# Layer 3's gates, inner convolutions and last products as 64x64 row halves inside the first scores of a frame

## The chip, the core and the metric

The kernel runs on one core of a Trainium2 chip. The metric is the device time of one execution in microseconds, as the median over runs of the same program. The core has a matrix engine (PE, with its weight loads listed apart as PEld), a vector engine (DVE), an activation engine (ACT), a general engine (POOL) and an engine that only synchronises and issues transfers (SP). Each engine works through its own queue; semaphores tie them together. Matrix products land in eight PSUM banks of 128 partitions by 2 KB.

## The reference

A residual stream x of 8 blocks of 512 tokens by 128 channels runs through four layers, each an attention-like part and a feed-forward part, everything in float32. The change is in layer 3, whose work the kernel interleaves with layer 2's attention. Cut to these:

```python
# layer 2, attention: 16 heads of width 64, softmax over the queries' axis
scores = jnp.einsum('bhqp,bhkp->bhqk', q, k) / jnp.sqrt(jnp.float32(P))
attn = jax.nn.softmax(scores, axis=2)
ctx = jnp.einsum('bhqk,bhkp->bqhp', attn, v)
out = concat(ctx) @ l_w.T + l_b

# layer 3, first part: a causal depthwise convolution of 21 taps, then two 128x128 products
return input_data @ W1 + h_hatt @ W2 + bias

# layer 3, second part: every operand rounded to FP4 in groups of 16
gate = fp4_linear(x, w_gate)          # 128 -> 352
y = fp4_linear(x, w_up)               # 128 -> 352
h = jax.nn.silu(gate) * y
return fp4_linear(h, w_down)          # 352 -> 128
```

Each part adds its result to x, and takes a layer norm of x as its input.

## The kernel before

**Frames.** From about 660 us on, the program is one loop over 64 frames (function `late`). Frame n handles one pair of layer 2's heads for one block: n // 8 is the block, n % 8 the pair. A frame's order, written out by hand, is: `scores(n, 0)`, `context(n - 1)`, `scores(n, 1)`, `project(n)`. The Tile scheduler is off (`tc.manual_schedule()`), so each engine's queue is in the order in which the statements are written.

- `scores(n, half)` makes the scores of two tiles of 128 keys. Each key tile is four 64x64 matmuls of 512 columns into a double bank (pool "two", two of them). DVE takes the negative maximum (L1589, tile `nm`), and ACT two exponentials for each key tile (L1595, tile `ex`). A double bank is free again once its two exponentials are done.
- `context(n - 1)` is eight matmuls with 128 rows and 64 columns of weights (`ex,vs`).
- `project(n)` makes the queries and keys of two frames ahead (`xt,blob_a`), the values (`blob_a,xt`) and the output product of the frame before (`blob_a,ct`). It is already cut into row halves on 64x64 tiles: while rows 0 to 63 of one product run, rows 64 to 127 of another do. Two row halves of one product add into the same bank, so the second must not start before the first has ended. `mark` puts an empty instruction on SP that waits for the last matmul of the first half, and the second half's first matmul waits for that. A half there is at most eight matmuls. Its two wide results lie in the two banks of pool "one"; ACT empties the queries' bank (L1498, tile `q`) and DVE the keys' (L1499, tile `k`).

**Layer 3 in the frames.** `planned(b, f0_)` hangs the steps of block b into the frames from f0_ on. A step has a place in its frame: "P" lies on PE behind both key tiles of `scores(n, 0)`, on ACT between the exponentials of its two key tiles; "V" comes after `scores(n, 0)`, "G" after `context`, "D" ahead of `project`, "E" at the end of the frame. Block b starts every eight frames, so the steps of two or three blocks lie in one frame. Blocks 0 to 5 run wholly in frames; the later steps of block 6 and all of block 7 are in `end()`, written out by hand behind the loop.

The steps that the change touches, in before:

- `gated(j)`, P, four times a block: gate and up product of one tile of 128 tokens, each one 128x128 matmul of 352 columns (L247, `wt_gate,xt` and `wt_up,xt`) into two banks of "one". ACT's tanh (L1884) reads the gate, `gated_v` on DVE (L1890, L1894) reads both.
- `conv_out`, E, once a block: eight matmuls of 128 columns into one bank, `xp` with W1 and `acc` (the taps' sum) with W2, then `added` on DVE (L1831), the next layer norm's `stats2` and, a place later, `scale2` on ACT (L1435).
- `turn_h(i)`, P, twice: transposes of the 352 columns of `h` in chunks of 128, 128 and 96 (L1925), and two copies for each tile of tokens on ACT (L1928, L1931).
- `down`, P, once: twelve matmuls of 128 columns (`wd,ht`) into one bank, then `added` and the store.

The PE list of one such frame reads: two key tiles, [P steps], context, two key tiles, project, [E steps].

Of the kernel before, what the change touches and what calls it, by code (L numbers as in the profile page):

```python
# [25 lines left out]
P = 128  # L26
D = 128
# [134 lines left out]
def body(ctx, tc, dram, spans, x_in, ib, it, ic, ei, out):  # L162
# [1176 lines left out]

    I3 = 352  # L1340
    chunks = [(0, P), (1, P), (2, I3 - 2 * P)]

    def fp4_scale(pool, src, blocks, bufs=1, room=None):

# [42 lines left out]
    def late():  # L1387
# [11 lines left out]
        with tc.tile_pool(name="a2", bufs=2) as wp, tc.tile_pool(name="l3", bufs=1) as lp:  # L1399
# [94 lines left out]
            def queries_out(n, pk, pq):  # L1494
# [4 lines left out]
                nc.vector.tensor_scalar(k, pk, a2["kb"][:, cc : cc + 1], None, ALU.add)  # L1499
                qks[n] = q, k  # L1500

            def project(n):

                b, cc = divmod(n + 1, 8)
                b2, cc2 = divmod(n + 2, 8)
                bo, co = divmod(n - 1, 8)
                pk, pq, pv = bank(), bank(), bank("c")
                pv = pv.rearrange("p (j n) -> p j n", j=J)
                if co == 0:
                    outs[bo] = bank("o")  # L1510
                po = outs[bo].rearrange("p (j d) -> p j d", j=J)
                ct, xq, xv = cts.pop(n - 1), xts[b2], xts[b]

                after = []

                def put(*args, **kw):
                    ins = nc.tensor.matmul(*args, **kw).ins  # L1517
                    if after:
                        tc.add_manual_dep(ins, after.pop().name, SYNC)
                    return ins  # L1520

                def mark(ins):

                    m = nc.sync.nop(nofuse=True).ins
                    tc.add_manual_dep(m, ins.name, SYNC)
                    return m

                def wide(ps, w, r, first):
                    for m in range(2):
                        at_ = cc2 * P + 64 * m  # L1530
                        put(
                            ps[64 * m : 64 * (m + 1), :],
                            a2[w][r, at_ : at_ + 64],
                            xq[r, :],
                            start=first,
                            stop=not first,
                        )

                def by_tokens(ps, src, w, r, start, stop):
                    for j in range(J):  # L1540
                        for m in range(2):
                            at_ = j * P + 64 * m
                            last = put(
                                ps[64 * m : 64 * (m + 1), j, :],
                                src[r, at_ : at_ + 64],
                                w[r, :],
                                start=start and j == 0,
                                stop=stop and j == J - 1,
                            )
                    return last  # L1550

                low, high = slice(0, 64), slice(64, P)
                wl, wv = cols(a2["l"], co), cols(a2["v"], cc)
                wide(pk, "k", low, True)
                one = mark(by_tokens(po, ct, wl, high, co == 0, False))
                wide(pq, "q", low, True)
                two = mark(by_tokens(pv, xv, wv, high, True, False))
                after.append(one)
                wide(pk, "k", high, False)
                by_tokens(po, ct, wl, low, False, co == 7)  # L1560
                after.append(two)
                wide(pq, "q", high, False)
                by_tokens(pv, xv, wv, low, False, True)
                queries_out(n + 2, pk, pq)
                if co == 7:
                    add_to_residual(bo, po)
                values_out(n + 1, pv)

            def scores(n, half, between=lambda: None):


                q, k = qks[n]
# [8 lines left out]
                for kt in tiles:  # L1581
                    ps = bank2()
                    for i in range(2):
                        r = slice(64 * i, 64 * (i + 1))
                        for m in range(2):
                            at_ = kt * P + 64 * m
                            mm(ps[64 * m : 64 * (m + 1), i, :], k[r, at_ : at_ + 64], q[r, :])
                    nm = wp.tile([P, 2], F32, tag="nm", name="nm", bufs=4)
                    nc.vector.tensor_reduce(nm, ps, AX.X, ALU.max, negate=True)  # L1589
                    made[kt] = ps, nm  # L1590
# [170 lines left out]
            def layer3(b, xp, tile_, part=(0, J), conv_bank="one", h_tag="h"):  # L1761
# [111 lines left out]
                def gated(j, at_end=False, thirds=True):  # L1873
# [6 lines left out]
                        pg, pu = two[:, 0, :], two[:, 1, :]  # L1880
                    mm(pg[:, :I3], cols(t["xt"], j - j0), wt["gate"])
                    mm(pu[:, :I3], cols(t["xt"], j - j0), wt["up"])
                    s = lp.tile([P, I3], F32, tag="s", name="s", bufs=2)
                    nc.scalar.activation(s, pg[:, :I3], AF.Tanh, scale=0.5)  # L1884
                    if at_end and thirds:
# [33 lines left out]
                def turn_h(i):  # L1919
                    h = tile_("h", h_tile)  # L1920
                    ht = tile_("ht", lambda: lp.tile([P, J, 3, P], F32, tag="ht", name="ht"))
                    for j in (2 * i, 2 * i + 1):
                        pt = bank()
                        for k, w in chunks:
                            nc.tensor.transpose(  # L1925
                                pt[:w, k * P : (k + 1) * P], h[:, j, k * P : k * P + w], ident
                            )
                        nc.scalar.copy(  # L1928
                            ht[:, j, :2, :], pt[:, : 2 * P].rearrange("p (i n) -> p i n", i=2)
                        )  # L1930
                        nc.scalar.copy(ht[:96, j, 2, :], pt[:96, 2 * P : 3 * P])  # L1931

                def down():
                    ht = tile_("ht", None)
                    po = bank()
                    for j in range(j0, j1):
                        for k, w in chunks:
                            mm(
                                cols(po, j),
                                ht[:w, j, k, :],  # L1940
                                wt["down"][:w, k, :],
                                start=(j == j0 and k == 0),
                                stop=(j == j1 - 1 and k == 2),
                            )
                    added(po)
                    nc.sync.dma_start(
                        out[b * TB + lo : b * TB + hi, :].rearrange("(j p) d -> p j d", p=P),
                        x[b][:, j0:j1, :],
                    )

                stats, scale, turn_, _ = norm_steps(
                    b, lambda: xp()[:, pad + lo : pad + hi], "b3", part
                )
                stats2, scale2, _, t2 = norm_steps(b, None, None, part)
                return SimpleNamespace(**{k: v for k, v in locals().items() if callable(v)})

            def planned(b, f0_):

# [1 line left out]


                soon = b < 2 or b == NB - 2
                z = 9 - soon
                plan = [
                    (1, "V", s.stats) if b < 2 else (0, "E", s.stats),
                    (1, "G", s.scale),
                    (1, "E", s.turn_),
                    (2, "V", lambda: s.conv_v(1, 2, 3, 4)),
                    (2, "G", lambda: s.conv_s(6, 7)),
                    (2, "E", lambda: s.conv_s(8, 9, 10)),  # L1970
                    (2, "D", lambda: s.conv_v(5)),
                    (3, "G", lambda: s.conv_s(11, 12)),
                    (3, "E", lambda: s.conv_s(13, 14, 15)),
                    (4, "G", lambda: s.conv_s(16, 17)),
                    (4, "E", lambda: s.conv_s(18, 19, 20)),
                    (5, "V", s.join),
                    (5, "E", s.conv_out),
                    (5, "E", s.stats2),
                    (6, "G", s.scale2),
                    (6, "E", s.quant_x1) if soon else (7, "V", s.quant_x1),  # L1980
                    (z - 1, "V", s.quant_x2),
                    (z - 1, "E", s.turn_x),
                ]
                for j in range(J):

                    g = z + j + int(b > 0 and j > 0)
                    plan.append((g, "P", lambda j=j: s.gated(j)))
                    plan.append((g, "V", lambda j=j: s.gated_v(j)))
                plan += [
                    (z + 2, "V", lambda: s.quant_h1(0)),  # L1990
                    (z + 3, "V", lambda: s.quant_h2(0)),
                    (z + 4, "V", lambda: s.quant_h1(1)),
                    (z + 5, "V", lambda: s.quant_h2(1)),
                    (z + 5, "P", lambda: s.turn_h(0)),
                    (z + 6, "P", lambda: s.turn_h(1)),
                    (z + 6, "E", s.down) if b > NB - 4 else (z + 7, "P", s.down),
                ]
                for frame, kind, f in plan:
                    at(f0_ + frame, kind, f)
                return s  # L2000
# [100 lines left out]
            def weights_in_frames():  # L2101
# [20 lines left out]
                def turned_w(name):  # L2122
                    ps = bank()
                    w_ = wq[name]
                    if name == "down":
                        for i, w in chunks:
                            nc.tensor.transpose(
                                ps[:w, i * P : (i + 1) * P], w_[:, i * P : i * P + w], ident
                            )
                        wt["down"] = const.tile([P, 3, P], F32, tag="wd", name="wd")  # L2130
                        nc.vector.tensor_copy(
                            wt["down"][:, :2, :], ps[:, : 2 * P].rearrange("p (i n) -> p i n", i=2)
                        )
                        nc.vector.tensor_copy(wt["down"][:96, 2, :], ps[:96, 2 * P : 3 * P])
                    else:
                        for i, w in chunks:
                            nc.tensor.transpose(
# [67 lines left out]
            with tc.manual_schedule():  # L2205
# [1 line left out]
                xts[0] = t[0]["next"]  # L2207
                queries(0)
                for n in range(N):
                    scores(n, 0, lambda: (n > 0 or (values(0), queries(1)), hook(n, "P")))  # L2210
                    if n - 1 in experts_after:
                        waiting()
                    hook(n, "V")
# [63 lines left out]
```

## Time and profile before

| what | value |
|---|---|
| median of 3 runs | 1434.34 us (1434.13 to 1439.14) |
| the profiled execution's own time | 1434.78 us |
| its span, first to last instruction | 1433.0 us |
| mean granted PE clock | 0.998 |
| PE busy in the span | 1372.8 us (96%) |
| ACT, DVE, POOL busy | 1041.7, 986.5, 622.1 us |
| PE busy from 886 to 1287 us | 399.6 of 401 us |

A timeline row gives the start in microseconds, the time to the end of its last instruction, engine, line, operation, tiles (out<-in), the shape, and how many instructions were merged; in brackets the idle time ahead of it and what ended it. `64*64` is rows by columns of the weights. A float32 matmul shows as two records. Neighbouring PE rows overlap, because a matmul's record lasts longer than the time until the next one can start: what a piece of PE work costs is read from start to start.

### The profile page before, as it was taken

The numbers are of one execution on the slowest core, as the hardware profiler recorded it, in microseconds if no ns is written. First come the engines' busy times: TensorE is split into PE (matmuls) and PEld (weight loads), VectorE is DVE, ScalarE is ACT, GpSimd is POOL, SyncE is SP. The second block draws the span as 40 slices with busy tenths as digits, with TensorE's granted clock in tenths as the row PEclk, the third lists the DMA queues.
The fourth block names the chain that finished last, engine by engine and source line by source line (L and its number), as shares of the span: only waits on it lengthen the run. The fifth ranks groups of instructions, "written<-read, shape, count | busy, mean of one in ns | idle before, by whom it ended". The sixth has DMA issues, their size and how long they took to land.

```text
span 1433.0 us, 31909 instructions
## 1 busy us (share of the span) xinstructions
PE 1372.8 (96%) x12498; PEld 703.9 (49%) x12498; DVE 986.5 (69%) x2072; ACT 1041.7 (73%) x2126; POOL 622.1 (43%) x726
## 2 busy tenths in 40 slices
PE   7889999999999999999999899999999999999997
PEld 3752222222377745534553455555555555555566
DVE  6776665676477777634671687886887877877876
ACT  7869999999887646655875577876866767768632
POOL 6746766666533533201620272442632633524423
PEclk9999999999999999999999999999999999999999
DMA  5039999988451010101000000000000000000000
GB/s 176 1 49 132 140 133 129 126 129 124 77 181 42 10 41 24 39 1 31 2 2 1 1 2 9 2 2 9 2 2 9 1 9 2 2 9 2 2 8 16
DMA packets 33272, 60.06 MB, mean 42 GB/s; under 512 B 5601, under 2 KB 25633, under 8 KB 28642
## 3 DMA queue, kind: packets, MB, share of 16 engines
q1 hardware_dynamic: 32416, 56.18, 22.2%
q8 instruction: 99, 1.62, 0.5%
q10 hardware_dynamic: 578, 1.57, 0.3%
q14 instruction: 51, 0.42, 0.1%
q0 software_dynamic: 128, 0.26, 0.1%
HBM read 49.70 MB, written 8.29 MB: 40 GB/s over the span
## 4 chain that ended last, share of the span: by engine, by line
PE 65%; ACT 18%; DVE 11%; DMA 2%; issue 2%; POOL 1%; SPq 0%; DVEq 0%; POOLq 0%; ACTq 0%
PE ps L247 50%; PE ps L1517 13%; ACT hm L565 8%; ACT hm L564 4%; ACT ex L1595 3%; DVE nm L1589 2%; DMA gs<-gates 1%; DVE s L723 1%; ACT h L385 1%; DVE s L1423 1%; ACT xn L1435 1%; PE ps L1453 1%; DMA gates<-eq 1%; POOL rs L244 1%; DVE fa L1375 0%
## 5 line engine op out<-in xcount | busy, mean ns | idle before, releaser
L1595 ACT ACTIVATE ex<-ps,nm 128x512 f32<-128x512 f32 x512 | 345.6, 687 | 150.4 <-DVE nm L1589 150.4
L1589 DVE TENSOR_REDUCE nm<-ps 128x2 f32<-128x1024 f32 x256 | 299.6, 1211 | 46.2 <-PE ps L247 45.7
L247 PE MATMUL ps<-q,k 64*64 64x512 f32 x2048 | 250.6, 600 | 6.6 <-ACT ex L1595 5.5
L247 PE MATMUL ps<-ex,vs 128*64 128x512 f32 x1024 | 233.8, 598 | 0.0
L1517 PE MATMUL ps<-xt,blob_a 64*64 64x512 f32 x976 | 222.2, 589 | 0.0
L583 POOL TENSOR_TENSOR acc<-acc,pr 128x512 f32<-128x512 f32 x119 | 166.8, 1401 | 104.7 <-DVE pr L577 96.0
L1610 POOL TENSOR_TENSOR vs<-v,sm 128x256 f32<-128x256 f32 x128 | 78.4, 613 | 295.1 <-DVE sm L1609 268.9
L565 ACT ACTIVATE hm<-ps,blob_f 128x1536 f32<-128x1536 f32 x128 | 196.2, 1533 | 0.0
L577 DVE SCALAR_TENSOR_TENSOR pr<-ps,blob_f,gs 128x512 f32<-128x512 f32 x120 | 90.0, 750 | 88.9 <-PE ps L247 70.9
L247 PE MATMUL ps<-h,w 32*128 32x512 f32 x1024 | 147.4, 639 | 1.5 <-ACT hm L564 0.6
L247 PE MATMUL ps<-hm,w 128*32 128x512 f32 x1024 | 136.2, 604 | 2.0 <-DVE pr L577 2.0
L247 PEld LDWEIGHTS ps<-ex,vs 128*64 128x64 f32 x1024 | 67.8, 136 | 142.5 <-issue 116.5
L247 PEld LDWEIGHTS ps<-q,k 64*64 64x64 f32 x2048 | 68.1, 132 | 140.6 <-issue 78.6
L1797 POOL TENSOR_TENSOR acs<-acs,prod 128x512 f32<-128x512 f32 x98 | 124.9, 1274 | 8.5 <-ACT prod L1796 3.6
L1517 PE MATMUL ps<-blob_a,xt 64*64 64x128 f32 x1952 | 126.9, 269 | 0.0
L1517 PE MATMUL ps<-blob_a,ct 64*64 64x128 f32 x1952 | 126.8, 269 | 0.0
L1517 PEld LDWEIGHTS ps<-blob_a,ct 64*64 64x64 f32 x1952 | 113.7, 133 | 0.0
L1517 PEld LDWEIGHTS ps<-blob_a,xt 64*64 64x64 f32 x1952 | 110.3, 133 | 0.0
L243 POOL TENSOR_SCALAR rs<-mv 128x4 f32<-128x4 f32 (+1 forms) x69 | 17.8, 258 | 211.4 <-DVE mv L1425 140.2
L1595 ACT ACTIVATION_READ_ACCUMULATOR ex<-ps,nm 128x1 f32 x512 | 105.3, 206 | 0.0
L564 ACT ACTIVATE hm<-ps,blob_f 128x512 f32<-128x512 f32 x128 | 88.0, 687 | 17.5 <-PE ps L247 17.5
L247 PEld LDWEIGHTS ps<-h,w 32*128 32x128 f32 x1024 | 40.7, 183 | 109.0 <-ACT hm L564 93.9
(316 smaller groups left out, 2204.8 us busy)
## 6 DMA issues: line engine op xcount, KB each, us to landing
gs<-gates SPq DMA_DIRECT2D x256, 128.0 KB
blob_f<-in_f SPq DMA_DIRECT2D x1, 2560.0 KB
blob_a<-in_a SPq DMA_DIRECT2D x1, 2056.0 KB
x<-in_x SPq DMA_DIRECT2D x8, 256.0 KB
gates<-eq SPq DMA_DIRECT2D x8, 256.0 KB
ge<-gates SPq DMA_DIRECT2D x4, 512.0 KB
back<-nought SPq DMA_DIRECT2D x7, 256.0 KB
by_rows<-fxn SPq DMA_DIRECT2D x7, 256.0 KB
```

Of the source, the lines that this page charges most:

```text
L243: nc.gpsimd.tensor_scalar(t, var, EPS, None, ALU.add)
L244: nc.gpsimd.tensor_tensor(t, t, half[:, : t.shape[-1]], ALU.pow)
L247: nc.tensor.matmul(out_, lhs, rhs, start=start, stop=stop)
L564: nc.scalar.activation(hm[:, 0, :], p1, AF.Gelu, bias=bias)
L565: nc.scalar.activation(hm[:, 1:, :], p3, AF.Gelu, bias=bias)
L577: nc.vector.scalar_tensor_tensor(pr, po, f0["b2"][:, e : e + 1], gs, ALU.add, ALU.mult)
L583: nc.gpsimd.tensor_tensor(acc[:, b, :], acc[:, b, :], pr, ALU.add)
L1517: ins = nc.tensor.matmul(*args, **kw).ins
L1589: nc.vector.tensor_reduce(nm, ps, AX.X, ALU.max, negate=True)
L1595: nc.scalar.activation(ex[kt][:, i, :], ps[:, i, :], AF.Exp, bias=nm[:, i : i + 1], accum_out=sm[:, kt, i : i + 1],)
L1610: nc.gpsimd.tensor_tensor(vs[:, tiles, :, :], vs_[n][:, tiles, :].rearrange("p j (i n) -> p j i n", i=2), sm[:, tiles, :].unsqueeze(3).to_ ...
L1797: nc.gpsimd.tensor_tensor(t["acs"], t["acs"], p, ALU.add)
```

## The change

1. **Gates on 64x64 tiles.** A new place "S" in `scores(n, 0)`: the first half of a step is issued between the two key tiles, the second half behind the second. `gate_steps(j)` issues gate rows 0 to 63 and up rows 64 to 127 as the first half, up rows 0 to 63 and gate rows 64 to 127 as the second. `in_halves` puts one `mark` between them. The evaluation is now `gate_out` and stays in P.
2. **Convolutions of blocks 2 to 5** (`conv_steps`) and **last products of blocks 0 to 4** (`down_steps`) go the same way through `token_steps`: two banks of two token tiles each; the first half is all of rows 0 to 63 for tiles 0 and 1 and then all of rows 64 to 127 for tiles 2 and 3. Their sums are added by two DVE instructions (`pair_added`) in place of one.
3. **The 352 columns of h in three overlapping runs of 120**, with the doubled weight rows set to zero, so that a run splits into 64 and 56 rows; one ACT copy for each transposed tile in place of two.
4. **Other frames.** The inner convolution moves from the end of frame 5 to S of frame 6, its statistics to P and its scaling to E of frame 6; the first gate of inner blocks moves one frame later; `turn_h` and the last product of blocks 1 to 4 move one frame later; tap 4 goes from V to D of frame 2 and tap 5 from D of frame 2 to D of frame 3.

```diff
+            def in_halves(first, second):
+                def a():
+                    m = mark(first()[-1])
+                    def b():
+                        tc.add_manual_dep(second()[0], m.name, SYNC)
+                    return b
+                return a
...
-            def scores(n, half, between=lambda: None):
+            def scores(n, half, between=lambda: None, more=()):
...
                             mm(ps[64 * m : 64 * (m + 1), i, :], k[r, at_ : at_ + 64], q[r, :])
+                    more = [f() for f in more]
                     nm = wp.tile([P, 2], F32, tag="nm", name="nm", bufs=4)
...
+                def gate_steps(j):
...
+                    def first():
+                        t["gate", j] = pg, pu = bank(), bank()
+                        return rows_(pg, "gate", low, True) + rows_(pu, "up", high, True)
+                    def second():
+                        pg, pu = t["gate", j]
+                        return rows_(pu, "up", low, False) + rows_(pg, "gate", high, False)
+                    return in_halves(first, second)
+                def token_steps(name, terms):
+                    def rows_(ps, js, half, first):
+                        made = []
+                        for i, j in enumerate(js):
+                            for k, (src, w) in enumerate(terms()):
...
+                                for m in range(2):
+                                    made.append(
+                                        nc.tensor.matmul(
+                                            ps[64 * m : 64 * (m + 1), i * P : (i + 1) * P],
+                                            s_[r, 64 * m : 64 * (m + 1)],
+                                            w_[r, :],
...
+                    def first():
+                        t[name] = a, c_ = bank(), bank()
+                        return rows_(a, (0, 1), 0, True) + rows_(c_, (2, 3), 1, True)
+                    def second():
+                        a, c_ = t[name]
+                        return rows_(c_, (2, 3), 0, False) + rows_(a, (0, 1), 1, False)
+                    return in_halves(first, second)
...
-                    (2, "V", lambda: s.conv_v(1, 2, 3, 4)),
+                    (2, "V", lambda: s.conv_v(1, 2, 3)),
...
-                    (2, "D", lambda: s.conv_v(5)),
+                    (2, "D", lambda: s.conv_v(4)),
...
+                    (3, "D", lambda: s.conv_v(5)),
...
-                    (5, "E", s.conv_out),
-                    (5, "E", s.stats2),
-                    (6, "G", s.scale2),
+                if inner:
+                    plan += [
+                        (6, "S", s.conv_steps()),
+                        (6, "P", lambda: s.pair_added("conv")),
+                        (6, "P", s.stats2),
+                        (6, "E", s.scale2),
+                    ]
...
-                    g = z + j + int(b > 0 and j > 0)
-                    plan.append((g, "P", lambda j=j: s.gated(j)))
+                    g = z + j + int(inner or (b > 0 and j > 0))
+                    plan.append((g, "S", s.gate_steps(j)))
+                    plan.append((g, "P", lambda j=j: s.gate_out(j, *s.t["gate", j])))
...
-                    (z + 5, "P", lambda: s.turn_h(0)),
-                    (z + 6, "P", lambda: s.turn_h(1)),
-                    (z + 6, "E", s.down) if b > NB - 4 else (z + 7, "P", s.down),
+                    (z + 5 + w, "P", lambda: s.turn_h(0)),
+                    (z + 6 + w, "P", lambda: s.turn_h(1)),
...
+                        (z + 7 + w, "S", s.down_steps()),
+                        (z + 7 + w, "V", lambda: (s.pair_added("down"), s.stored())),
```

## The prediction

> **What bounds the kernel now.** I read the page first. Its first line puts PE far ahead of the others:
>
> ```profile
> PE 1372.8 (96%) x12498; PEld 703.9 (49%) x12498; DVE 986.5 (69%) x2072; ACT 1041.7 (73%) x2126; POOL 622.1 (43%) x726
> ```
>
> In the frames it is tighter still: 399.6 of 401 us from 886 to 1287. So time saved on PE in a frame counts in full, as long as no other engine is late. The timeline of PE, three stretches: a frame with a gate, one around an inner convolution (frame 38), one with a last product.
>
> ```profile
> 1020.76 1.90 PE L247 MATMUL ps<-q,k 64*64 64x512 f32 x16
> 1022.59 0.86 PE L247 MATMUL ps<-wt_gate,xt 128*128 128x352 f32 x2
> 1023.28 0.76 PE L247 MATMUL ps<-wt_up,xt 128*128 128x352 f32 x2
> 1023.97 3.65 PE L247 MATMUL ps<-ex,vs 128*64 128x512 f32 x16
> ...
> 1044.98 1.16 PE L247 MATMUL ps<-blob_l,xp 128*128 128x128 f32 x8
> 1045.98 1.06 PE L247 MATMUL ps<-blob_l,acc 128*128 128x128 f32 x8
> 1046.96 1.95 PE L247 MATMUL ps<-q,k 64*64 64x512 f32 x16
> 1048.84 0.87 PE L1925 MATMUL ps<-blob_c,h 128*128 128x128 f32 x6
> 1049.65 3.65 PE L247 MATMUL ps<-ex,vs 128*64 128x512 f32 x16
> ...
> 1072.94 2.94 PE L247 MATMUL ps<-wd,ht 128*128 128x128 f32 x24
> 1075.82 0.65 PE L247 MATMUL ps<-ex,vs 128*64 128x512 f32 x2
> ```
>
> Start to start, a gate costs 1023.97 - 1022.59 = 1.38 and a last product 2.88. Scores and context follow each other without a hole.
>
> ACT's timeline at two frame starts shows when the queries' bank comes free:
>
> ```profile
> 1020.99 0.69 ACT L1498 ACTIVATE q<-ps,qb 128x512 f32<-128x512 f32 x1
> ...
> 1033.32 0.70 ACT L1498 ACTIVATE q<-ps,qb 128x512 f32<-128x512 f32 x1
> ```
>
> That is 0.92 behind the first scores at 1020.76, and 1.24 behind those at 1032.78. Next, the weight loads inside a `project`, which tell how far PE looks ahead:
>
> ```profile
> 1006.49 0.47 PEld L1517 LDWEIGHTS ps<-blob_a,xt 64*64 64x64 f32 x8
> 1006.83 0.14 PEld L1517 LDWEIGHTS ps<-blob_a,ct 64*64 64x64 f32 x2
> 1006.93 0.14 PEld L1517 LDWEIGHTS ps<-xt,blob_a 64*64 64x64 f32 x2
> ```
>
> The `ct` pair is for rows 0 to 63, whose tiles could take new weights from 1006.56 on (start of the queries' second matmuls). It comes 0.27 later, with the last of the `xt` loads for rows 64 to 127, although those rows' own next loads wait till 1006.93. In program order, ten instructions ahead of the first `ct` load and thirteen ahead of the second were then unissued; one step (0.109) earlier, four more. The trace has the same offsets in all 52 `project`s. I read it as a window: an instruction overtakes at most thirteen unissued ones. Last, DVE in frame 38:
>
> ```profile
> 1047.07 0.69 DVE L1831 TENSOR_TENSOR x<-x,ps 128x512 f32<-128x512 f32 x1 [0.93 <-PE ps L247]
> 1049.06 2.35 DVE L1589 TENSOR_REDUCE nm<-ps 128x2 f32<-128x1024 f32 x2
> 1051.32 0.86 DVE L1423 BATCH_NORM_STATS2 s<-x 128x6 f32<-128x128 f32 x4
> 1055.54 2.32 DVE L1589 TENSOR_REDUCE nm<-ps 128x2 f32<-128x1024 f32 x2
> 1057.83 0.75 DVE L1499 TENSOR_SCALAR k<-ps,blob_a 128x512 f32<-128x512 f32 x1
> ```
>
> There DVE runs without a hole for eleven microseconds: in these frames it is the second bound.
>
> **Gates: 24 in frames.** `project` does four groups of 64x64 tiles by 512 columns in 3.46, so 0.866 a group and 0.595 for 352 columns; two halves 1.19 in place of 1.38: -0.19. But the first half stands one key tile (0.87) behind the frame's start where the old gate stood two behind it, and takes both banks of "one". Its up product gets the queries' bank, so its load waits for the copy at L1498 plus 0.10 (0.05 from an ACT end to the PE load released by it, as at the `xt` copy ending 753.73, and 0.05 for the load). Behind the waiting load PE's queue holds key tile 1, and the lag lasts to `context`, which needs all rows. With the copy ending at 0.92 the wait is 0.92 + 0.10 - 0.87 = 0.15; at 1.24, 0.47. Gate 0 of each block and gate 1 of block 0 find the bank free: 7 x -0.19 = -1.3. Gates 1 and 2 of blocks 1 to 5: 10 x (-0.19 + 0.15) = -0.4. Their gates 3, where the copy ends at 1.22 to 1.24 in every block: 5 x (-0.19 + 0.47) = +1.4. Block 0's gates 2 and 3, where ACT is later still (copies end 1.85 and 1.86 behind the scores at 806.83 and 820.40): about +0.8 and +0.4. Sum +0.9; the ends are -4.6 (no wait) and +2.5. The marker's way (0.15 from a record's end to SP's event at 1006.48) fits behind key tile 1, and no store stands ahead of it on SP: nothing.
>
> **Last products: 5.** Eight `project` matmul records in two columns take 0.435, so 0.109 a step. A half here is 24 records a row half, 12 steps, 1.31. If both row halves ran together: 2 x 1.31 = 2.62 against 2.88, -0.26. But all 48 instructions of rows 0 to 63 are queued first. Four issue per step, and the other rows' first load gets within thirteen unissued ones at the ninth step: 8 x 0.109 + 0.05 = 0.92 late. The same holds at each change of rows behind so long a run. From the frame's start: low rows 0.87 to 2.18, high rows from 1.79 to 3.10; key tile 1's low rows from 2.71 to 3.58; second half's low rows to 4.89, its high rows from 4.50 to 5.81. The two key tiles alone are 1.73, so the product costs 4.08: +1.2 each, +6.0 in all. Ends -1.3 and +6.5. The adds and the store move to V; DVE has holes in these frames (1.35 ahead of the old add).
>
> [...]
>
> **Inner convolutions: 4.** Here a row half has 32 instructions: the high rows start 4 x 0.109 + 0.05 = 0.49 behind the low ones, but their bank is the queries', whose copy at the end of frame 37 is late (ends 1.5 behind 1044.98). Counted from `project`'s last matmul (1044.81), with gate 3 having cost PE 0.3: bank free at 1.5; first half 0.87 to 2.37, key tile 1 to 3.24, second half to 4.2, context at 4.3. The old way: 1049.65 - 1044.81 less 0.80 of transposes, now a frame later, = 4.04. So PE alone +0.25. Then DVE: after key tile 1 it has a maximum (1.17), both adds (0.8), both statistics (1.3 each) and the rounding (2.9) ahead of the third maximum: 3.4 + 7.5 = 10.9, where the old row stands at 10.7 (1055.54) though PE is now 0.7 ahead. Two maxima and two pairs of exponentials (1.35 each) later the double banks come free at 13.6 and 14.9; PE wants them at 13.1 and 13.9. It stands in frame 39 some 0.5 and 0.5, where before it lost 0.33 (scores 2.16 at 1058.46 against 1.83). Context of frame 39 comes at 16.7, as before (16.6), but with 0.8 of transposes still to do: +0.85 in each of frames 30, 38 and 46. In frame 54 the other block's statistics are missing: +0.25. Sum +2.8; ends 0 and +5.
>
> **The rest.** Transposes keep count and columns. One ACT copy in place of two ends each `turn_h` about 0.1 earlier; in frames the exponentials hide that, in `end()` PE waits for it: -0.2 (0 to -0.4).
>
> **Sum.** +0.9 + 6.0 + 2.8 - 0.2 = +9.5 on the profiled execution's 1434.78 (span 1433.0 and 1.8 around it), which is 0.4 above the median: 1434.3 + 9.5 = 1443.8.
>
> **Rivals.**
> *The rows overlap in full* (the other side). The window is no limit for matmuls whose tiles are free. [...] For it: `ct` matmuls at 1006.99 do pass four waiting ones. Against: the constant offsets. Last products -1.3 in place of +6.0, convolutions +2.5: 1434.3 + 0.9 - 1.3 + 2.5 - 0.2 = 1436.2, not measurably slower.
> *The banks are free in time.* Gates save all 4.6: 1438.3 with the window, 1430.7 without. For it: PE waits nowhere for `q` in steady frames now. Against: the copy can't start before the queries' last matmul ends.
> *DVE and ACT fall further behind*, and stalls of 0.5 spread to two more frames a block: 1449.
> [...]
>
> **How the numbers follow.** Forecast 0.46; rows overlap 0.19, banks free 0.10, both 0.13; DVE 0.08; drains 0.04. A measurement of this kernel can tell about 0.5%, 7.2 us, from no change. Forecast alone spans 1439 to 1448: above 1441.5 with 0.34 of its 0.46; with the last two cases that makes slower 0.46. Of the 0.13 for both free, 0.11 is for convolutions and key tiles gaining too, below 1427.2: faster 0.11. The rest, 0.43, is the same. Range 1429 to 1449.
>
> **What would show it.** Right: `wd,ht` rows from first to second row half 0.9 apart, 4.1 a product; PE idle in front of `wt_up` ended by ACT `q`; scores behind frame 38 over 2.5. Wrong: both row halves of `wd,ht` starting within 0.1, or gate frames 0.19 shorter each.

## The result and the profile after

| | before | after |
|---|---|---|
| median | 1438.05 us (6 runs beside those of after) | 1445.06 us (6 runs, 1443.83 to 1450.06) |
| ratio | | 1.0064, 95% interval 1.0041 to 1.0087 |
| profiled execution | 1434.78 us, span 1433.0 | 1444.44 us, span 1442.3 |

The changed kernel is 0.6% slower: 9.66 us between the profiled executions, where 9.5 was predicted. Ahead of the first frame two executions can differ by over 5 us (it starts at 507.15 us in the trace of after, at 512.74 in that of `turns_by_term`), so a part is priced here inside the frames: from the start of one frame's `context` on PE to the start of the next, where untouched frames of two executions agree within 0.02 almost everywhere. From the first context to the last, after is 10.0 longer than before. (The first frame of the loop starts at 507.75 us in the trace of before, not at 660.)

The first line of the page after:

```profile
PE 1380.9 (96%) x13338; PEld 724.0 (50%) x13338; DVE 995.2 (69%) x2081; ACT 1042.1 (72%) x2094; POOL 624.0 (43%) x726
```

PE has 840 matmul records more and 8.1 us more work; DVE has 8.7 us more, ACT 0.4. PE's timeline, frame 37 (gate 3 of block 3) and frame 41 (the last product of block 3); lines have moved by 2 to 22 (L1500 is the old L1498, L1539 the old L1517):

```profile
1035.77 1.04 PE L247 MATMUL ps<-q,k 64*64 64x512 f32 x8
1036.63 0.76 PE L1978 MATMUL ps<-wt_gate,xt 64*64 64x352 f32 x4
1037.31 0.51 PE L1978 MATMUL ps<-wt_up,xt 64*64 64x352 f32 x2
...
1039.50 1.08 PE L247 MATMUL ps<-ex,vs 128*64 128x512 f32 x4
...
1086.87 1.09 PE L247 MATMUL ps<-q,k 64*64 64x512 f32 x8
1087.78 2.09 PE L2009 MATMUL ps<-wd,ht 64*64 64x128 f32 x42
...
1090.51 2.41 PE L2009 MATMUL ps<-wd,ht 64*64 64x128 f32 x48
1092.85 0.65 PE L247 MATMUL ps<-ex,vs 128*64 128x512 f32 x2
```

In frame 37 the gate's and the up product were to start together, as two products of `project` do (1005.28 and 1005.29 in before); the up product starts 0.68 later. The weight loads name what it waits for, ACT's copy of the queries, which ends 1.49 behind the scores (1.24 in before):

```profile
1036.56 0.70 ACT L1500 ACTIVATE q<-ps,qb 128x512 f32<-128x512 f32 x1
...
1037.31 0.14 PEld L1978 LDWEIGHTS ps<-wt_up,xt 64*64 64x64 f32 x2 [0.53 <-ACT q L1500]
```

In frame 41 a half should take 1.31, as worked out in the prediction. From its first record to the context the second half takes 2.34. A merged row has the form of its first instruction; by single records the 56-row matmuls start 0.886 behind the 64-row ones in both halves, and the first half keeps the upper rows from key tile 1 until 1090.02, 2.24 behind its own start.

Frame 38 holds a convolution. DVE's timeline behind it, and the scores of frame 39:

```profile
1052.89 0.74 DVE L2031 TENSOR_TENSOR x<-x,ps 128x256 f32<-128x256 f32 x2
1053.55 0.86 DVE L1425 BATCH_NORM_STATS2 s<-x 128x6 f32<-128x128 f32 x4
...
1054.80 0.86 DVE L1425 BATCH_NORM_STATS2 s<-x 128x6 f32<-128x128 f32 x4
...
1059.02 2.32 DVE L1605 TENSOR_REDUCE nm<-ps 128x2 f32<-128x1024 f32 x2
```

```profile
1061.75 1.09 PE L247 MATMUL ps<-q,k 64*64 64x512 f32 x8
1063.09 1.09 PE L247 MATMUL ps<-q,k 64*64 64x512 f32 x8 [0.25 <-ACT ex L1611]
```

```profile
1061.75 0.21 PEld L247 LDWEIGHTS ps<-q,k 64*64 64x64 f32 x8 [0.38 <-ACT ex L1611]
```

DVE works without a hole from the maximum at 1051.75 to the one at 1059.02, 10.71 behind the frame's scores (1048.31) and 10.81 behind the last matmul of `project` (1048.21), from which the forecast counted 10.9. The exponentials behind it release the double banks late: the load of frame 39's first key tile waits 0.38 for them, and its two key tiles stand 1.34 apart instead of 0.87.

### The profile page after: what moved, and what is told of

Read it like the earlier page. It is cut to its first block, busy times and chain, and to the rows that moved or that the text cites. A ratio compares the mean times of both kernels' runs of the same rounds, so it can differ in the third digit from the quotient of the medians.

```text
span 1442.3 us, 33570 instructions
## 1 busy us (share of the span) xinstructions
PE 1380.9 (96%) x13338; PEld 724.0 (50%) x13338; DVE 995.2 (69%) x2081; ACT 1042.1 (72%) x2094; POOL 624.0 (43%) x726
## 3 DMA queue, kind: packets, MB, share of 16 engines
q10 hardware_dynamic: 578, 1.57, 0.3%
## 4 chain that ended last, share of the span: by engine, by line
PE 65%; ACT 18%; DVE 11%; DMA 3%; issue 2%; POOL 1%; SPq 1%; DVEq 0%; POOLq 0%; ACTq 0%
PE ps L247 46%; PE ps L1539 12%; ACT hm L565 7%; ACT hm L564 3%; ACT ex L1611 3%; PE ps L1978 2%; PE ps L2009 2%; DVE nm L1605 2%; DMA gs<-gates 2%; DVE s L723 1%; ACT h L385 1%; ACT xn L1437 1%; DMA gates<-eq 1%; DVE s L1425 1%; SPq L545 1%
## 5 line engine op out<-in xcount | busy, mean ns | idle before, releaser
L247 PE MATMUL ps<-q,k 64*64 64x512 f32 x2048 | 265.1, 601 | 5.8 <-ACT ex L1611 4.5
L1539 PE MATMUL ps<-xt,blob_a 64*64 64x512 f32 x976 | 222.2, 589 | 0.0
L247 PEld LDWEIGHTS ps<-q,k 64*64 64x64 f32 x2048 | 74.1, 132 | 124.3 <-issue 81.8
L1539 PE MATMUL ps<-blob_a,ct 64*64 64x128 f32 x1952 | 126.9, 269 | 0.0
L1539 PE MATMUL ps<-blob_a,xt 64*64 64x128 f32 x1952 | 126.9, 269 | 0.0
L1539 PEld LDWEIGHTS ps<-blob_a,ct 64*64 64x64 f32 x1952 | 113.7, 133 | 0.0
L1539 PEld LDWEIGHTS ps<-blob_a,xt 64*64 64x64 f32 x1952 | 110.3, 133 | 0.0
```

Of the source, the lines that this page charges most:

```text
L247: nc.tensor.matmul(out_, lhs, rhs, start=start, stop=stop)
```

## The experiments

### One part at a time

`gates_alone` takes from the change only places and halves of the gates; `products_alone` only the last products; `conv_alone` has the convolutions and the moved frames of after, but gates and products as 128x128 tiles in P. All three keep the runs of 120 columns and the single ACT copy of a transposed tile, which takes some 0.3 to 0.4 off the frames in each.

```diff
 # conv_alone, against after
-                    plan.append((g, "S", s.gate_steps(j)))
-                    plan.append((g, "P", lambda j=j: s.gate_out(j, *s.t["gate", j])))
+                    plan.append((g, "P", lambda j=j: s.gated(j)))
...
-                        (z + 7 + w, "S", s.down_steps()),
-                        (z + 7 + w, "V", lambda: (s.pair_added("down"), s.stored())),
+                    plan.append((z + 7 + w, "P", s.down))
```

> Only the 24 gates go between the key tiles; convolutions, last products and the frames of all steps are as before (the three runs of 120 columns stay). Theory (each gate saves 0.2 on PE, and loses it again where the up product waits for ACT's copy of the queries): by the steps seen in the trace of after, 7 x -0.2, 10 x -0.05, 5 gates 3 x +0.52, block 0's last two together +0.2, tail -0.2: +0.6 us on the profiled execution before. Rival 1 (banks free in time): -4.6. Rival 2 (gate 3 became so late through the moved convolution and transposes, not by its own second half): gates 3 at +0.28, -0.6 in all, and the wait ahead of wt_up in frame 37 is 0.45 rather than 0.67.

> Only the five last products go between the key tiles, in the frames of before; gates and convolutions as before. Theory (the other rows' first load must come within thirteen unissued instructions, and 48 are queued ahead of it): 4.1 in place of 2.88 for each, high rows 0.89 behind the low ones in both halves: +6.1 us in all, tail -0.2. Rival 1 (rows overlap when nothing else is moved): 2.62 for each, -1.5 in all. Rival 2 (half of the loss is from the moved frames): about +3.

> Only the four inner convolutions go between the key tiles, with the frames of after for all steps; gates and last products are in P as 128x128 tiles, as before. Theory (DVE's chain of two adds, statistics and maxima binds behind the convolution): +0.8 in each of frames 30, 38, 46, +0.3 in 54, tail -0.2: +2.5 us. Rival (DVE is only late because gates and products around it make it so): PE's own +0.25 for each is left, +0.8 in all.

| kernel | frames against before | ratio, 95% interval |
|---|---|---|
| `gates_alone` | +0.4 us | 1.0005, 0.9992 to 1.0019 |
| `products_alone` | +6.4 | 1.0048, 1.0030 to 1.0067 |
| `conv_alone` | +4.0 | 1.0031, 1.0017 to 1.0044 |

The products lose all of it alone: +1.23 in each of four frames, +1.73 for block 0's; both rivals fall. The gates are near nothing, as by the theory, but with another share-out: gate 3 costs +0.32, not the +0.53 it has in after, and block 0's last two +0.84 and +0.16. The theory's price for gate 3 was wrong there and rival 2's was nearer (what made the gate later in after is the next section's question). The up product's load says the same (it was forecast at 0.45 behind the gate's):

```profile
1033.57 0.14 PEld L1978 LDWEIGHTS ps<-wt_gate,xt 64*64 64x64 f32 x2 [0.29 <-issue]
1034.04 0.14 PEld L1978 LDWEIGHTS ps<-wt_up,xt 64*64 64x64 f32 x2 [0.33 <-ACT q L1500]
```

`conv_alone` came out worse than either expectation. The convolutions cost +1.23, +1.20, +1.08 and +0.70 with the moved transposes and products, the five frames of gate 3 +0.12 each although those gates are old, and frame 20 is 0.78 *shorter*. So something that moved with the convolution makes two kinds of frames of other blocks different. And the parts alone sum to 10.8, with the gain of the single ACT copy counted three times; after has 10.0. The difference lies in the convolution frames: against before they are 0.53 shorter in after and 0.09 here. The same late copy of the queries is paid once: it ends 1.81 behind the scores of frame 38 here and 1.38 in after, where PE has already been held at gate 3, and the context comes 4.74 and 4.32 behind them.

### What moved with the convolution: tap 5

```diff
-                    (2, "V", lambda: s.conv_v(1, 2, 3)),
+                    (2, "V", lambda: s.conv_v(1, 2, 3, 4)),
...
-                    (2, "D", lambda: s.conv_v(4)),
+                    (2, "D", lambda: s.conv_v(5)),
...
-                    (3, "D", lambda: s.conv_v(5)),
```

> After, with taps 4 and 5 in their places of before (4 in V and 5 in D of frame 2). Theory (gate 3 costs +0.53 in place of the +0.32 it has alone because tap 5 now stands on DVE ahead of the keys' copy of frame 35 and its like, and everything behind it, up to the exponentials ahead of the queries' copy, comes later): frames 29, 37, 45, 53, 61 are 0.2 shorter each, and frame 20, which the moved tap made 0.8 shorter, gets that back; the rest as in after. Rival (the convolution's moved statistics or the moved transposes do it): these frames stay at +0.53.

This is one execution (1448.06 us), compared inside the frames alone. Against after, frames 29, 37, 45, 53 and 61 are 0.19 to 0.21 shorter, frame 20 is 0.80 longer, and no other frame differs by over 0.03. The theory holds in every number: the queries' copy ends 1.29 to 1.31 behind the scores of those five frames, against 1.48 to 1.50 in after and 1.28 to 1.30 in `gates_alone`. Frame 20 gains in after since its scores no longer wait for ACT's exponentials (0.84 in before, 0.64 here). The tap in after, with the keys' copy behind it, and what POOL does then; third, the same tap put back:

```profile
1022.15 1.74 DVE L1798 SCALAR_TENSOR_TENSOR acc<-xp,blob_l,acc 128x512 f32<-128x512 f32 x1
1023.81 0.74 DVE L1501 TENSOR_SCALAR k<-ps,blob_a 128x512 f32<-128x512 f32 x1
```

```profile
1020.71 2.63 POOL L1813 TENSOR_TENSOR acs<-acs,prod 128x512 f32<-128x512 f32 x2
```

```profile
1014.76 0.74 DVE L1798 SCALAR_TENSOR_TENSOR acc<-xp,blob_l,acc 128x512 f32<-128x512 f32 x1
```

Beside POOL's sum the tap takes 1.74 instead of 0.74, and pushes the keys' copy, the maxima and, a frame on, ACT's queries back. That holds for the moved taps of blocks 2 to 6 (1.74 in each, beside POOL's sum); those of blocks 0 and 1 begin when 0.67 and 1.02 of a sum are left, not 1.19, and take 1.21 and 1.57. All seven end 0.55 behind the sum that they met. The 28 taps in blocks 0 to 6 of before lie beside no POOL instruction of any kind and take 0.74 to 0.75.

### How far PE looks ahead

The same matmuls, banks and frames as in after; only the order inside a half differs. `turns_by_term` issues two matmuls (8 instructions) of one row half, then two of the other; `turns_by_tile` six (24) in a last product and four (16) in a convolution. In after it is 48 and 32.

```diff
-                        return rows_(a, (0, 1), 0, True) + rows_(c_, (2, 3), 1, True)
+                        return in_turn(rows_(a, (0, 1), 0, True), rows_(c_, (2, 3), 1, True))
...
+                    def in_turn(a, c_):
+                        made, run = [], 2     # by tile: 2 * len(terms())
+                        while len(made) < 8 * len(terms()):
+                            for rows in (a, c_):
+                                made += [next(rows) for _ in range(run)]
+                        return made
```

> After, but convolutions and last products issue their two row halves in turns of two matmuls (one token tile, one term: 8 instructions), not each half as one run; the same matmuls, banks and frames. Theory (thirteen unissued instructions is what an instruction overtakes): both row halves start within 0.05, a product costs 2.62 in place of 4.10, -7.4 us against after for the five; the convolutions' halves shorten by up to 0.5 on PE, of which DVE's chain and the queries' copy leave 0 to 0.3 each, 0 to -1.2. In all -7.4 to -8.6: 1436.5 to 1437.7 beside 1445.1, within 0.3% of before. Rival (a change between 64 and 56 rows, or between row groups, drains PE): twelve changes in a half in place of one, products stay at 4.1 or grow, no gain or slower than after.

> After, with the row halves issued in turns of one token tile: six matmuls (24 instructions) in a last product, four (16) in a convolution. Theory (an instruction overtakes at most thirteen unissued ones, four issue per step of 0.109): the high rows' first load gets within thirteen after (24 - 13) / 4, so three steps or less: 0.26 behind the low rows, against 0.89 with 48 queued and 0.01 with 8; a product costs 2.62 + 0.25 = 2.87, 1.23 less than in after, frames 33, 41, 49, 57 -1.2 each, block 0's about -0.9: -5.8 in all. [...] Rival 2 (strict order, no overtaking of waiting instructions): high rows 6 x 0.109 = 0.65 behind, product well over 3.2.

| instructions queued ahead of the other rows | frames 33, 41, 49, 57 against after | a last product |
|---|---|---|
| 48 (after) | 0 | 4.10 |
| 24 (`turns_by_tile`) | -1.21 | 2.89 (2.87 expected) |
| 8 (`turns_by_term`) | -1.48 | 2.62 (2.62 expected) |

PE's timeline of the product of block 3, first by term, then by tile:

```profile
1090.90 1.49 PE L2007 MATMUL ps<-wd,ht 64*64 64x128 f32 x48
...
1093.07 1.50 PE L2007 MATMUL ps<-wd,ht 64*64 64x128 f32 x48
1094.49 1.08 PE L247 MATMUL ps<-ex,vs 128*64 128x512 f32 x4
```

```profile
1085.96 1.54 PE L2007 MATMUL ps<-wd,ht 64*64 64x128 f32 x44
...
1088.13 1.76 PE L2007 MATMUL ps<-wd,ht 64*64 64x128 f32 x48
1089.82 1.08 PE L247 MATMUL ps<-ex,vs 128*64 128x512 f32 x4
```

By term both row halves run in one row of 48 records that lasts 1.49, where after's second half lasts 2.41. Twelve changes of rows in a half cost nothing that shows, so the rival of a drain falls; between 24 and 8 instructions lie 0.27 a product. By tile the upper rows start 0.23 behind the lower ones in the first half and 0.29 in the second (0.26 expected; 0.65 in strict order). Block 0's product gains 1.01 and 1.02. In all the frames are 7.0 shorter by term (7.4 to 8.6 expected) and 6.0 by tile (5.8). The convolutions moved by -0.13 and +0.13: the banks and DVE set those frames, not PE. In time: by term 1.0026 of before (1.0008 to 1.0044; median 1439.11), by tile 1.0048 (1.0023 to 1.0073; 1443.06).

Matmuls started ahead of older ones, too: in the trace of before the `ct` matmuls at 1006.99 come ahead of four that stand before them in the program, at 1007.04 and 1007.47. That an instruction overtakes at most thirteen was the author's estimate from the offsets in `project`; no run shows the count itself, only the three lengths of the table, with 1.48 a product between 8 and 48.

### What gate 3 and the convolution wait for

```diff
 # queries_on_dve: for the project ahead of gate 3 of blocks 1 to 5
+                if vector:
+                    nc.vector.tensor_scalar(q, pq, 0.125, qb[:, cc : cc + 1], ALU.mult, ALU.add)
...
 # stats_later: blocks 5 to 7
-                at(n, "V", stats)
+                at(n, "E" if b > 4 else "V", stats)
```

> After, but the queries that the banks of gate 3 of blocks 1 to 5 wait for are emptied by DVE, behind the keys' copy, and not by ACT behind the exponentials. Theory (gate 3 loses 0.72 to that one copy): DVE is free from about 0.1 behind the scores' start and takes 0.75, so the bank is free at 1.0 in place of 1.48; the wait ahead of wt_up falls from 0.67 to 0.2, frames 29, 37, 45, 53, 61 -0.5 each, -2.4 in all. Rival 1 (what holds PE there is the marker between the halves or a drain): no change. Rival 2 (DVE cannot carry it: its maxima come 0.7 later and the convolution frame behind loses it again): frames 30 and 38 +0.5, no change in all.

> After, with the next block's statistics (1.26 of DVE) moved from V to E of frames 30, 38 and 46, so out of DVE's chain behind the convolution. Theory (that chain is what frames 31, 39 and 47 wait for): their scores' stalls go, -0.5, -0.5, -0.37, -1.3 in all if nothing is late behind the new place. Rival (the stalls come from ACT's exponentials or from PE's later convolution): no change. Second rival (the statistics only move the lag on): frames 32, 40, 48 take it, no change in the sum.

`queries_on_dve`: gate 3's frames are 0.50 to 0.52 shorter, and the frames behind four of them 0.10 to 0.11 longer. The up product starts 0.18 behind the gate (forecast 0.2):

```profile
1040.69 0.46 PE L1982 MATMUL ps<-wt_gate,xt 64*64 64x352 f32 x2
1040.87 0.51 PE L1982 MATMUL ps<-wt_up,xt 64*64 64x352 f32 x2
```

Taking the copy off ACT takes the wait away, so the wait was for that copy; rival 1 falls, and rival 2 holds for a fifth of the gain. -2.1 in the frames of 1445 us is less than the times resolve (1.0046 of before, 1.0023 to 1.0069).

`stats_later`: frames 31, 39 and 47 are 0.84 shorter, more than the forecast 0.5, which counted only the gap between the key tiles (the wait ahead of the first one goes too), and frames 32, 40 and 48 take 0.22 back: -1.9 (ratio 1.0060, 1.0036 to 1.0083). DVE's chain was what these frames waited for, by way of the exponentials behind it; the second rival accounts for a quarter. Frame 39's scores then run through:

```profile
1061.82 1.90 PE L247 MATMUL ps<-q,k 64*64 64x512 f32 x16
```

### Two versions built from the prices

`mended` is after with the three repairs at once. `free_banks_only` is before, with the runs of 120 columns, and with only those steps moved that find their banks free or, as gates 1 and 2, wait 0.15:

```diff
+                    if j < (3 if b else 1):
+                        plan.append((g, "S", s.gate_steps(j)))
+                        plan.append((g, "P", lambda j=j: s.gate_out(j, *s.t["gate", j])))
+                    else:
+                        plan.append((g, "P", lambda j=j: s.gated(j)))
...
+                elif b == 0:
+                    plan.append((z + 7 + w, "P", s.down))
```

> After with the three repairs that the single runs priced, all at once: row halves in turns by term (-6.9 in the frames), the queries of gate 3 emptied by DVE (-0.4 x 5 = -2.0 with what the next frame gives back), the next block's statistics in E of frames 30, 38, 46 (-0.62 x 3 = -1.9). Theory (the terms are separate and add): after's frames are 9.9 above before's, so 9.9 - 10.8 = -0.9 from the first frame on beside before, and 1432.7 beside 1433.6 for the lowest of the runs. Rival (DVE, which two of the repairs load, takes part of it back): +0.5 to +2.

> Before, with only those steps between the key tiles that find their banks free: gates 0 to 2 of blocks 1 to 5, gate 0 of block 0, and the last products of blocks 1 to 4 with the row halves in turns by term; gate 3, block 0's other gates and last product, and the convolutions stay 128x128 in P, all steps in the frames of before. Theory: 6 x -0.2 for gates 0, 10 x -0.05 for gates 1 and 2, 4 x -0.26 for the products (2.62 against 2.88), tail -0.25: -3.0 beside before, some 1432 to 1433 for the median, 0.2% faster. Rival (the steps that were left out made room for these: DVE or ACT is late in frames where it was not): gates 0 to 2 at +0.15 each, no gain.

`mended`: -1.3 in the frames (-0.9 expected), median 1434.87, ratio 0.9990 (0.9978 to 1.0003): the three add up to a little more than their single prices (10.0 less 11.0 makes -1.0), and undo all that after had lost. `free_banks_only`: -2.5 in the frames (-3.0 with the tail expected): gates 0 at -0.20, gates 1 and 2 at -0.05, three of the four products at -0.25, the last at -0.10 (why it gives less is not shown); median 1432.98 beside 1435.38, lowest 1431.15 beside 1433.65, ratio 0.9989 (0.9975 to 1.0003). Its frames are the shortest of all, but its gain of 0.1 to 0.2% is not told from none by the interval.

## Why the prediction was right, and which terms were not

| step | predicted | in after | alone |
|---|---|---|---|
| gates with free banks (7) | -1.3 | -1.2 | -1.2 |
| gates 1 and 2 of blocks 1 to 5 | -0.4 | -0.5 | -0.5 |
| gates 3 of blocks 1 to 5 | +1.4 | +2.6 | +1.6 |
| block 0's gates 2 and 3 | +1.2 | +0.1 | +0.9 |
| last products | +6.0 | +6.7 | +6.7 |
| inner convolutions | +2.8 | +2.5 | see above |
| tail | -0.2 | -0.2 | -0.2 |
| sum | +9.5 | +10.0 | |

- **The last products** went as worked out: high rows 0.89 late (0.92), a product 4.10 (4.08), and nothing else in those frames. Block 0's was not worked out by itself: it starts 1.47 behind the scores instead of 0.91 (`products_alone`, where PE idles 0.38 ahead of `wd,ht` for the queries' copy); that is the 0.5 that it costs more.
- **Gates 0 to 2**: what a gate 0 saves (0.20 for 0.19) and what is left of it in gates 1 and 2 (0.05 for 0.04) were right to 0.01. Gate 1 of block 0 is the exception: it finds its banks free, but the frame is not shorter (0.00 for 0.19).
- **Gates 3** is the term that was mis-sized: +0.28 a gate predicted, +0.53 measured. Its mechanism was right, and so was its size as long as the change is the gates alone (+0.32). The step that failed is the queries' copy, taken to end 1.24 behind the scores, as in the trace of before. In after it ends 1.48 to 1.50 behind them, because "4. Other frames" of the change moves tap 5 into DVE's way one frame earlier; the prediction passed over the taps without a price. Tap and POOL's sum together cost 0.2 a block there, which `taps_back` returns.
- **Block 0's gates**: alone +0.84 and +0.16 (predicted +0.8 and +0.4); in after the same move of the taps gains 0.8 in frame 20. The taps thus changed two terms, by +1.0 and by -0.8, and the sum came out nearly untouched. That the total was right to 0.5 owes something to this, and to the last products (+0.7) and the convolutions (-0.3), which missed on opposite sides: it is in part luck.
- **The convolutions**: the chain on DVE was right. Counted as in the forecast, from the last matmul of `project`, the third maximum comes at 10.81 (10.9), the context at 4.42 (4.3), frame 39's two key tiles at 13.54 and 14.88 (13.6 and 14.9). The mark of "scores behind frame 38 over 2.5" was missed, 2.36: the first of the two stalls lies ahead of the scores' first record, where their length does not show it. Both together are 0.84 (`stats_later`) in place of 1.0, so the first three convolutions cost 0.78, 0.78 and 0.64 in place of 0.85, and that of frame 54 +0.27 (+0.25).
- **The rivals**: rows that overlap in full (0.886 apart in after, 0.01 only when issued in turns) and banks free in time (the up product 0.68 behind the gate) are each decided by a run. The forecast gave 0.04 to drains of PE at 56-row weights; no run shows one, and a product with twelve changes of rows in a half takes 2.62. DVE and ACT did not fall further behind: the frames that are longer are those of the steps in the table, of the transposes moved with them, and the one behind each convolution.

## What to carry to other kernels

When two halves of PE are to run beside each other, issue them in turns of few instructions: here the other half started 0.886 behind with 48 instructions queued ahead of it, 0.23 and 0.29 with 24, and 0.01 with 8. Price every line of a plan that moves, also the ones that only make room; here a vector instruction moved by one frame changed gates of another block by 0.2 and 0.8. A step that fits into PE's order may still not fit the order in which its banks come free, so ask for each of its instances which copy ends last.

## What the runs showed of the hardware

- PE started matmuls ahead of older ones (in before the `ct` matmuls at 1006.99 ahead of four, at 1007.04 and 1007.47), and a product took longer the more instructions of one row group were queued ahead of the other: with 8, 24 and 48 the same matmuls take 2.62, 2.89 and 4.10. The count of thirteen, an estimate from the offsets in `project`, gave 2.62, 2.87 and 4.08 in advance. Only these three lengths were run.
- Weights of 56 rows beside those of 64: their changes cost nothing that shows (in `turns_by_term` a half with 24 records in either row group takes 1.31, from 1090.90 to key tile 1 at 1092.21).
- A moved tap on DVE takes up to 1.74 beside POOL's sum, and the 28 taps of before, with no POOL instruction beside them, 0.74 to 0.75. POOL's sums lie at 1020.71 to 1023.34 and the tap ends 0.55 behind them, as the other six moved taps do behind theirs. What makes the tap longer is not shown.
